# Second pass of a two-layer kernel: keys and values projected behind the unit's query, convolution taps dealt from one list of counts

## Chip, cores and metric

The kernel runs on one core of one Trainium2 chip, in float32. The time is device microseconds of one execution. Before the change three runs took 3788.51, 3795.89 and 3799.6 us, so the median is 3795.89 us.

## What is computed

Two layers follow each other on x of shape (8, 32, 32, 512).

```python
# layer 0: group norm, attention with 8 heads of 64 over 1024 tokens, output projection, residual
# layer 1, with B = 8 images of 1024 tokens and C = 512 channels:
q_img   = layernorm(x) @ wq + bq                        # as an image, channels first
o       = gelu(depthwise_conv7x7_stride2(q_img) + dw_b) # 16 x 16 points
points  = grid + tanh(conv1x1(o))                       # where to sample
smp     = bilinear_sample(x, points)                    # 256 samples of 512 channels
k = v   = smp @ wv + bv
kh, vh  = k @ mk_w + mk_b,  v @ mv_w + mv_b
qh      = q @ mq_w + mq_b
z       = softmax(qh kh^T) vh @ mo_w + mo_b + x         # 8 heads
out     = gelu(layernorm(z) @ mlp_w + mlp_b) + z
```

So in layer 1 an image's convolution must end before its samples can be gathered, and its samples before its keys and values are there. The chain of image b+1 runs while the attention of earlier images is computed.

## The kernel before, in words

**Two passes.** Layer 0 is the first pass; it ends some 2198 us into the profiled execution and is not touched. Layer 1 is the second pass (from line 776 on). There the projections of the reference are folded (`wvk`, `wvv`, `wqq`), and the work is cut into 64 **units**: image b has units 8b to 8b+7, for two halves of its tokens (`hi`) times four pairs of heads (`hp`).

**An order written out by hand.** Every step is put on a list with `at(place, step)` (line 347), where place is a unit's number and a fraction. `run_due` sorts by place and issues all steps in that order; `InOrder` keeps the program order on each engine. TensorE (PE), VectorE (DVE), ScalarE (ACT), GpSimd (POOL) and SyncE (SP, which issues DMAs) each run their own instructions in this order.

**A unit** n, in the order of its places:

- `scores` (n): 16 matmuls `sc<-keys,q`; DVE takes the negated maximum (`nmax<-sc`, two reductions), ACT the exponentials `e`. Then `product` of unit n-1 (`av<-et,vals`), `scale` (DVE, `attH`), and at n+0.17 `query_step` of the next unit (`mm<-hat_h,wqq`).
- From unit 4 on, the **tail of an earlier half**, one token tile t a unit (`back_steps`, line 1027): `joined` (`mm<-wo,attH`, then on DVE `z<-mm,xr`, `stats`, `mv`, with a power on POOL), `norm` (`zn`), `turned` (`mm<-ident,zn`), `mlp` (`mm<-wm,zT`), `biased` (DVE, `res<-mm,bm_row`), then for two tiles at a time Gelu on ACT and on POOL an addition and the store (`end`), followed by POOL's additions `xr<-xr,bo_row` (`add`) for the next two.
- `fill` (`mm<-wq_r,hat`): half a channel block of the query image; `fill_end` adds the bias into a padded image (`pad<-mm,bq_row`, on DVE). There are two padded images (`PADS`), used in turn by the four channel blocks of each image.
- `share` (DVE), the transposes `transposed` 0 and 1 (`mm<-ident,e`), `turn` (`mm<-ident,rep`).
- **Taps**: 49 multiply-adds a channel block, `o<-pad,dww,o`, all on DVE, 196 an image.

**PSUM.** All projections and transposes take their output from one ring of three tiles (`ps_mm`, line 268). The fourth allocation after a given one is issued only when the engine that empties the earlier tile has done so. Counted along a unit, the tile of `turned`, or of a key or value projection put ahead of it, is that of `fill`, which DVE empties with `pad<-mm,bq_row`.

**The steps that are moved.** `conv_steps` (line 1119) places fills and taps of image b over eight units, 8b-12 to 8b-5, in counts (23, 13, 29, 30, 28, 24, 25, 24); for b = 1 over units 0 to 3, 49 each. Then come Gelu, `offsets` (16 matmuls `mm<-pww,o`), `targets` (26 small DVE instructions), `gather` (four indirect DMAs from POOL, twice) and `sample` (four DVE instructions, twice). `key_step` (line 1007, `mm<-smp,wvk`, 8 matmuls) is placed four times at 8b-1.4, 8b-1.2, 8b+0.8 and 8b+2.2, `value_step` (line 1013, `mm<-wvv,smp`, 8 matmuls) twice at 8b-0.4 and 8b+0.6. In the order of PE these places lie between the transposes of e and `turned` (0.6), or between `mlp` and `turn` (0.8), except the one at 8b+2.2, which lies behind the query (n+0.17) and ahead of `joined` (n+0.46).

## Time and profile before

| | us |
|---|---|
| runs, median of three | 3795.89 |
| profiled execution, its own time | 3789.67 |
| its span in the trace | 3788.0 |
| TensorE busy over the span | 3578.3 |
| VectorE busy | 2789.1 |
| ScalarE busy | 1529.3 |
| GpSimd busy | 750.6 |
| units 0 to 3 (to the first matmul of unit 4) | 120.5 |
| units 4 to 13 | 246.8 |
| units 14 to 21 (and each eight after them, to unit 45) | 194.5 |
| units 46 to 51 | 150.7 |
| units 52 to 62 | 228.6 |
| unit 63 and the end | 64.5 |

A unit's length is the distance between the first `sc<-keys,q` matmuls of two units in the timeline of PE. Matmuls overlap, so work is best measured from start to start. A line of the timeline has the start, the length, the engine, the operation, what it writes and reads, the number of instructions in a run, and in brackets the idle time ahead of it with the instruction that ended it. In the view by stretches a row has the bounds, the length, then busy time and number of instructions for PE, PEld, DVE, ACT and POOL, the granted clock of TensorE, and the DMA share.

### The profile page before, as it was taken

The numbers are of one execution on the slowest core, as the hardware profiler recorded it, in microseconds if no ns is written. First come the engines' busy times: TensorE is split into PE (matmuls) and PEld (weight loads), VectorE is DVE, ScalarE is ACT, GpSimd is POOL, SyncE is SP. The second block draws the span as 40 slices with busy tenths as digits, with TensorE's granted clock in tenths as the row PEclk, the third lists the DMA queues.
The fourth block names the chain that finished last, engine by engine and source line by source line (L and its number), as shares of the span: only waits on it lengthen the run. The fifth ranks groups of instructions, "written<-read, shape, count | busy, mean of one in ns | idle before, by whom it ended". The sixth has DMA issues, their size and how long they took to land.

```text
span 3788.0 us, 46075 instructions
## 1 busy us (share of the span) xinstructions
PE 3578.3 (94%) x16152; PEld 1868.9 (49%) x16152; DVE 2789.1 (74%) x4264; ACT 1529.3 (40%) x3218; POOL 750.6 (20%) x838
## 2 busy tenths in 40 slices
PE   8999999999999999999998787999999999999997
PEld 4554554545545455455453434454545454544543
DVE  5678777776777777867766569898988888888333
ACT  3443443433434434344364123343434343444443
POOL 0003012020030120301346201121121212121212
PEclk9999999999999999999999898999999999999999
DMA  5667666665666666655755501021111111110100
GB/s 154 155 158 188 164 168 170 162 184 153 162 189 159 170 168 163 188 155 150 199 143 143 176 1 67 34 71 41 67 45 56 56 56 56 56 56 34 59 23 31
DMA packets 235350, 438.23 MB, mean 116 GB/s; under 512 B 49296, under 2 KB 53392, under 8 KB 232176
## 3 DMA queue, kind: packets, MB, share of 16 engines
q1 hardware_dynamic: 212528, 363.08, 35.4%
q0 software_dynamic: 21440, 70.11, 5.8%
q8 instruction: 129, 2.11, 0.2%
q10 hardware_dynamic: 1152, 2.10, 0.2%
q14 instruction: 101, 0.83, 0.1%
HBM read 115.84 MB, written 50.86 MB: 44 GB/s over the span
## 4 chain that ended last, share of the span: by engine, by line
PE 69%; DVE 20%; issue 6%; DMA 1%; ACT 1%; POOL 1%; SPq 0%; DVEq 0%; POOLq 0%; ACTq 0%
PE mm L53 42%; PE sc L53 15%; PE av L53 13%; DVE o L53 10%; DVE nmax L53 3%; DVE stats L53 1%; DVE sq L53 1%; DVE pad L53 1%; POOL mv L53 1%; ACT e L53 1%; DVE z L53 1%; DVE zn L53 1%; DVE attH L53 1%; DVE mv L53 1%; DMA row<-mid,ii 0%
## 5 line engine op out<-in xcount | busy, mean ns | idle before, releaser
L53 ACT ACTIVATE e<-sc,nmax 128x1024 f32<-128x1024 f32 (+1 forms) x1024 | 804.6, 799 | 901.8 <-DVE nmax L53 901.3
L53 DVE TENSOR_REDUCE nmax<-sc 128x1 f32<-128x1024 f32 (+1 forms) x640 | 753.2, 1219 | 481.5 <-PE sc L53 480.3
L53 DVE SCALAR_TENSOR_TENSOR o<-pad,dww,o 128x256 f32<-128x256 f32 x1344 | 721.3, 537 | 44.1
L53 DVE STREAM_TRANSPOSE sq<-e 128x1024 f32<-128x1024 f32 x512 | 608.1, 1226 | 50.8 <-ACT e L53 49.5
L53 PE MATMUL sc<-k,q 64*128 64x512 f32 x2048 | 527.3, 618 | 13.5 <-ACT q L53 6.2
L53 PE MATMUL av<-et,v 128*64 128x256 f32 x4096 | 504.2, 389 | 16.3 <-DMA et<-sq 9.4
L53 PE MATMUL mm<-xT,wqkv 128*128 128x512 f32 x1024 | 471.5, 604 | 2.6 <-issue 2.6
L53 PEld LDWEIGHTS av<-et,v 128*64 128x64 f32 x4096 | 276.0, 138 | 322.9 <-issue 177.2
L53 POOL TENSOR_TENSOR mv<-mv,minus_half 128x1 f32<-128x1 f32 x128 | 74.3, 581 | 1396.3 <-DVE mv L53 1334.1
L53 PEld LDWEIGHTS sc<-k,q 64*128 64x128 f32 x2048 | 181.6, 186 | 276.2 <-issue 229.8
L53 PEld LDWEIGHTS mm<-xT,wqkv 128*128 128x128 f32 x1024 | 185.9, 191 | 226.8 <-issue 219.7
L53 ACT COPY et<-mm 128x512 f32<-128x512 f32 x256 | 140.7, 593 | 317.6 <-PE mm L53 317.4
L53 PE MATMUL mm<-wqkv,xT 128*128 128x128 f32 x2048 | 244.5, 278 | 0.0
L53 PEld LDWEIGHTS mm<-wqkv,xT 128*128 128x128 f32 x2048 | 233.8, 192 | 19.9 <-issue 19.9
L53 PE MATMUL mm<-wm,zT 128*128 128x512 f32 x512 | 240.4, 613 | 2.9 <-ACT zT L53 2.9
L53 PE MATMUL mm<-hat_h,wqq 128*128 128x512 f32 x512 | 236.7, 605 | 0.0
L53 PE MATMUL mm<-wo,attH 128*128 128x512 f32 x512 | 231.4, 595 | 3.1 <-DVE attH L53 3.1
L53 PE MATMUL mm<-wout,attT 128*128 128x512 f32 x512 | 233.7, 601 | 0.0
L53 ACT ACTIVATION_READ_ACCUMULATOR e<-sc,nmax 128x1 f32 x1024 | 209.2, 204 | 0.0
L53 PE MATMUL mm<-wq_r,hat 128*128 128x512 f32 x448 | 203.8, 598 | 0.2 <-ACT et L53 0.2
L53 PE MATMUL mm<-ident,e 128*128 128x128 f32 x1024 | 152.6, 293 | 26.7 <-DVE z L53 11.4
L53 PEld LDWEIGHTS mm<-hat_h,wqq 128*128 128x128 f32 x512 | 92.1, 189 | 143.0 <-issue 131.6
(153 smaller groups left out, 3629.5 us busy)
## 6 DMA issues: line engine op xcount, KB each, us to landing
et<-sq SPq DMA_DIRECT2D x2048, 128.0 KB, 2.7
xr<-in_x_dram POOLq DMA_DIRECT2D x64, 256.0 KB, 3.7
hat_h<-hat_d SPq DMA_DIRECT2D x16, 1024.0 KB, 5.3
xr<-mid SPq DMA_DIRECT2D x64, 256.0 KB, 3.1
out_dram<-res POOLq DMA_DIRECT2D x64, 256.0 KB, 2.3
x<-in_x_dram POOLq DMA_DIRECT2D x60, 256.0 KB, 3.8
mid<-xr SPq DMA_DIRECT2D x56, 256.0 KB, 2.9
hat_d<-hat SPq DMA_DIRECT2D x56, 256.0 KB, 2.9
```

Of the source, the lines that this page charges most:

```text
L53: return self.tc.keep_in_program_order(op(*args, **kwargs))
```

## The change

The convolutions of all images get their places from one list of counts per unit: image 1 over five units (40, 40, 39, 39, 38), image 2 over seven (19, 26, 27, 27, 32, 32, 33), and images 3 to 7 over eight as before, in other counts. Fills take the last two free slots (n+0.49) ahead of a block's first tap. Where only one slot is free, both go into one unit, 0.26 apart. `point_steps` then places Gelu to sample by the unit in which the last tap stands (5 for image 1, 8b-4 for the others, as before). Keys go to 8b-1.82, 8b-1.81, 8b+1.18 and 8b+2.18, values to 8b-0.82 and 8b+0.18, that is right behind `query_step` in units 8b-2 (two keys), 8b-1 (value), 8b (value), 8b+1 (key), 8b+2 (key). For image 1 the first two keys come at 7.18. No instruction is added or removed.

```diff
-        def conv_steps(b):
-            last = 2 * NHP * b - NHP
-            each = 1 if b == 1 else 2
-            first = last - NC * each
...
-            for n, count in enumerate((49,) * NC if each == 1 else (23, 13, 29, 30, 28, 24, 25, 24)):
...
+        def conv_counts():
+            units = [40, 40, 39, 39, 38]
+            units += [19, 26, 27, 27, 32, 32, 33]
+            for _ in range(3, B):
+                units += [25, 13, 25, 31, 26, 28, 23, 25]
+            return units
...
+        def conv_steps():
+            chunks, filled = conv_places(), -2
+            for k, places in enumerate(chunks):
+                b, cb = 1 + k // NC, k % NC
+                if cb == 0 and b > 1:
+                    at(max(int(places[0]) - 2.45, filled + 0.02), lambda b=b: conv_fetch(b))
+                free = max(filled, chunks[k - PADS][-1] if k >= PADS else filled)
+                slots = [n + 0.49 for n in range(-1, 60) if free < n + 0.49 < places[0] - 0.05]
+                slots = slots[-2:] if len(slots) > 1 else [slots[0], slots[0] + 0.26]
+                filled = slots[1]
...
+                if cb == NC - 1:
+                    point_steps(b, int(places[-1]) + 1)
+
+        def point_steps(b, last):
             at(last - 0.035, lambda: conv_gelu(b))
...
-            for hp, place in enumerate((2.6, 2.8, 4.8, 6.2)):
-                at(last + place, lambda hp=hp: key_step(b, hp))
-            for t, place in enumerate((3.6, 4.6)):
-                at(last + place, lambda t=t: value_step(b, t))
+            first = 2 * NHP * b
+            for hp, place in enumerate((-1.82, -1.81, 1.18, 2.18)):
+                at(max(first + place, last + 2.18), lambda hp=hp: key_step(b, hp))
+            for t, place in enumerate((-0.82, 0.18)):
+                at(first + place, lambda t=t: value_step(b, t))
...
-        for b in range(1, B):
-            conv_steps(b)
+        conv_steps()
```

Within a unit the taps keep their fractions: 45% of a unit's count between 0.26 and 0.46, which is ahead of `joined` on DVE, the rest behind `share`.

More of the change, by code (lines that the diff above doesn't have):

```diff
@@ L1117, in unit_steps, with conv_places @@
                 at(n + 0.17, lambda: query_step(*divmod(n + 1, NHP)))
-        def conv_steps(b):
-            last = 2 * NHP * b - NHP
-            each = 1 if b == 1 else 2
-            first = last - NC * each
-            if b > 1:
-                at(first - 2.45, lambda: conv_fetch(b))
-            for cb in range(NC):
-                for par in range(2):
-                    n, frac = divmod(par * each, 2)
-                    n = first + cb * each - each + (par if each == 2 else 0)
-                    frac = 0.49 if each == 2 or par == 0 else 0.75
-                    if (b, cb) == (2, 0):
-                        n, frac = first - 1, 0.49 + 0.3 * par
-                    at(n + frac, lambda cb=cb, par=par: fill(b, cb, par))
-                    at(n + frac + 0.04, lambda cb=cb, par=par: fill_end(cb, par))
-            i = 0
-            for n, count in enumerate((49,) * NC if each == 1 else (23, 13, 29, 30, 28, 24, 25, 24)):
+        def conv_counts():
[4 more added lines that the diff above has]
+            return units
+        def conv_places():
+            places = []
+            for n, count in enumerate(conv_counts()):
                 for j in range(count):
@@ L1141, in conv_steps @@
                     x = 0.26 + 0.2 * x / 0.45 if x < 0.45 else 0.57 + 0.36 * (x - 0.45) / 0.55
-                    at(first + n + x, lambda i=i: tap(b, *divmod(i, KS * KS)))
-                    i += 1
+                    places.append(n + x)
+            taps = KS * KS
+            return [places[i : i + taps] for i in range(0, len(places), taps)]
+        def conv_steps():
[8 more added lines that the diff above has]
+                filled = slots[1]
+                for par, place in enumerate(slots):
+                    at(place, lambda b=b, cb=cb, par=par: fill(b, cb, par))
+                    at(place + 0.04, lambda cb=cb, par=par: fill_end(cb, par))
+                for i, place in enumerate(places):
+                    at(place, lambda b=b, cb=cb, i=i: tap(b, cb, i))
+                if cb == NC - 1:
+                    point_steps(b, int(places[-1]) + 1)
+        def point_steps(b, last):
             at(last - 0.035, lambda: conv_gelu(b))
```

## Prediction

> **What bounds the kernel now.** First the page: which engine is full, and where.

> ```profile
> PE 3578.3 (94%) x16152; PEld 1868.9 (49%) x16152; DVE 2789.1 (74%) x4264; ACT 1529.3 (40%) x3218; POOL 750.6 (20%) x838
> ...
> DVE  5678777776777777867766569898988888888333
> ...
> PEclk9999999999999999999999898999999999999999
> ```

> The second pass is the last 17 slices. VectorE is at 8 to 9 tenths there and drops to 3 when the convolutions are done; TensorE stays near 9. Two engines are close to full, so the question is how they wait for each other. Next the stretches (units 0 to 3, 14 to 21, 53 to 62):

> ```profile
> 2198.50:2319.00 120.50, 88.10 (x281) 44.06 (x280) 105.00 (x208) 27.96 (x87) 2.88 (x2) 0.85 0.09 35
> ...
> 2565.90:2760.40 194.50, 184.06 (x707) 97.64 (x706) 169.36 (x323) 80.35 (x211) 38.13 (x40) 0.98 0.16 55
> ...
> 3515.80:3723.40 207.60, 191.20 (x769) 103.32 (x768) 69.73 (x119) 98.11 (x256) 42.67 (x46) 0.98 0.12 41
> ```

> Units 0 to 3 are VectorE's, the last ones TensorE's, and in the eight units that repeat both are nearly full, TensorE with 10.4 us idle. Then PE's timeline of unit 14, the longest of the eight (30.6 us), and DVE's beside it:

> ```profile
> 2576.64 3.60 PE L53 MATMUL mm<-wq_r,hat 128*128 128x512 f32 x8
> 2580.07 0.60 PE L53 MATMUL mm<-ident,e 128*128 128x128 f32 x4
> 2581.93 0.66 PE L53 MATMUL mm<-ident,e 128*128 128x128 f32 x4 [1.26 <-DVE z L53]
> 2584.88 3.78 PE L53 MATMUL mm<-smp,wvk 128*128 128x256 f32 x8 [2.29 <-DVE pad L53]
> 2588.46 1.05 PE L53 MATMUL mm<-ident,zn 128*128 128x128 f32 x4
> ```

> ```profile
> 2570.77 10.24 DVE L53 SCALAR_TENSOR_TENSOR o<-pad,dww,o 128x256 f32<-128x256 f32 x13
> ...
> 2581.19 0.68 DVE L53 TENSOR_TENSOR z<-mm,xr 128x512 f32<-128x512 f32 x1
> ...
> 2584.14 0.68 DVE L53 TENSOR_TENSOR pad<-mm,bq_row 128x512 f32<-128x512 f32 x1
> ```

> The key projection stands where its PSUM tile is the fill's, and waits until DVE, behind 14 taps, has emptied it. Without the key, `turned` would wait for the same `pad`. So the key is work that TensorE has in hand and does after the wait instead of before it. The view of waits puts 49.1 us in 34 places on `pad` from unit 4 on.

> **Durations, from start to start.** All from PE's and DVE's timelines of units 12 to 20. A tap costs 0.513 (16 in 8.2), but even units lose 3.2 more: from 2570.77 to `z` at 2581.19 14 taps took 10.42 where 7.2 are due, because POOL's second store addition and its two `add`s (2.7 to 9.6 us into the unit) each hold a tap up; if taps start after 6.2, only the `add`s remain, 2.4. Key 1.82, value 3.54, `offsets` 1.70, targets 3.1, one `sample` 2.76. PE reaches `joined` at 7.33, `fill` ends at 14.36, `turned` would start at 15.15, and from `turned` to the unit's end 5.40 pass. On DVE, nmax starts at 2.03 or when the unit before is finished (its lag d); taps start 2.87 later; `z` to the start of `pad` 2.95; `turned` follows `pad` by 0.74; the second part of the taps by 1.17, and `res` ends DVE's unit after 0.60 more.

> With these few terms I walk along both queues unit by unit: `z` = nmax + 2.87 + taps (or `joined`, if later), `pad` = z + 2.95 (or the fill, if later), `turned` = the later of TensorE's own place and pad + 0.74. For units 12 to 19 before the change the walk gives 192.1; measured 194.5. The rest is the halved clock in unit 14, where a key took 3.58 instead of 1.82 and the unit 2.6 more than walked. So the walk holds to 1 us in eight units.

> **1. Keys and values behind the query, units 14 to 45.** Each puts `joined`, `fill` and `turned` back by its own length and gives DVE that time. The walk for the new counts:

> - unit 12 (25 taps, offsets): lag 2.3, `pad` 17.5, `turned` 18.2 for a place of 16.85; length 23.6, lag after it 5.4
> - 13 (13 taps, two samples): `pad` 17.1, `turned` 17.8 for 15.15; 23.2
> - 14 (two keys): `turned` at its own place 18.79, no wait; 24.2 (was 30.6)
> - 15 (value): 18.69, no wait; 24.1 (24.7), lag 4.3 from 31 taps
> - 16 (value, 12 + 14 taps): z = 4.3 + 2.87 + 12 x 0.513 + 2.4 = 15.8, `pad` 18.7, `turned` 19.5 for 15.15 + 3.54 = 18.69; length 19.5 + 5.4 = 24.9 (29.1); lag 18.7 + 1.17 + 14 x 0.513 + 0.6 - 24.9 = 2.8
> - 17 (key): 16.97, no wait; 22.4 (20.6)
> - 18 (key): 17.9 for 16.97; 23.3 (23.6)
> - 19: no wait; 20.55 (20.57)

> The sum is 186.2. The wait in unit 13, 2.65, is put at half clock for one window, 1.7: 187.9 for 194.5, so 6.6 less, four times: **-26.4**. The instructions moved are 48 matmuls and six evacuations on ACT per image; they queue behind the query's evacuation, done 5.7 us after nmax starts, when ACT is idle for 4 us. A key behind the query (7.33) takes the tile of `res` of the unit before, so it would wait for DVE beyond a lag of 7.3; the walk's largest is 5.4. DMAs of these steps: none.

> [...]

> ```profile
> 2580.20:2583.60 3.40, 1.13 (x9) 0.65 (x7) 2.67 (x7) 1.17 (x2) 0.51 (x1) 1.00 0.17 62
> 2634.80:2638.20 3.40, 1.85 (x10) 0.92 (x8) 2.74 (x7) 1.17 (x2) 0.40 (x1) 1.00 0.00 0
> 3611.00:3614.40 3.40, 1.15 (x11) 0.91 (x10) 2.60 (x7) 1.07 (x2) 0.55 (x1) 1.00 0.24 77
> ```

> After the first and third, a third busy, the clock is 0.5; after the second, 54% busy, it stays; no single gap is over 2.3. So I count about 2.05 us idle within one 3.4 us window as the limit, and unit 13 falls under it. [...]

> **2. Units 46 to 51.** The same up to 49 (24.2, 24.1, 24.9, 22.4); 50 and 51, without fills, stay at 24.4 and 20.3: 140.3 for 150.7, **-10.4**.

> **3. Units 52 to 62, a loss.** There are no fills and taps, and `turned` waits for `zn`, which follows `joined` at a fixed distance. A key or value between the two covers that wait:

> ```profile
> 3589.09 3.71 PE L53 MATMUL mm<-wvv,smp 128*128 128x512 f32 x8
> ...
> 3613.89 0.66 PE L53 MATMUL mm<-ident,zn 128*128 128x128 f32 x4 [2.25 <-DVE zn L53]
> ```

> Moved ahead of `joined`, it no longer does: units 54, 55 and 56 get the wait of 2.3. A unit is then 19.42, ten of them 194.2, four keys and two values 14.4, halved clock in four or five (3 of 7 such units before) 7.2: 215.8 for 207.6, **+8.2**. [...]

> **4. Units 0 to 13.** DVE sets the pace at first: nine taps fewer a unit (4.65) and a `pad` (0.6) fewer in two units bring unit 4's nmax from 2331.7 to 2311.9. But 38 taps of image 1 are left, with two fills in that unit: the second comes behind `mlp`, and its `pad` makes DVE wait about 4.3, and the next query 1.2 for the tile of `res`. From there the walk gives 23.5, 28.7, 27.7, 24.7, 22.5, 28.5, 25.3, 25.0, 24.9 for units 5 to 13: 6 (z = 2.1 + 2.87 + 12 x 0.513 + 2.76 + 3.2 = 17.1, `turned` 20.8 for 15.15) and 10 stand 5.7 and 4.0 us on DVE and get the halved clock (2 to 2.5 each, as unit 4), 7 is PE's (two keys and a value), 11 has two fills again. Unit 4 ends at 2339.2, so unit 14 starts at 2570.0 for 2565.9: **+4.1**. Nothing near shows such units, so from both sides: without halved clocks -5, with two windows each +11. I take +4.1, since unit 14's row, with 3.55 idle, did halve. The image's fetch (8 us to land) now waits in SP's queue for unit 3's second fill, 2299, and lands at 2307, ahead of its fill at 2316; behind it in that queue are only row fetches for unit 5. Unit 5's gathers stand ahead of POOL's additions, which end at 11.5 of unit 6; `z` comes at 17.

> **Sum.** -26.4 - 10.4 + 8.2 + 4.1 = -24.5. Span 3788.0 gives 3763.5, the profiled execution 3789.67 gives 3765.2, and the median of the runs 3795.89, 6 above it, gives 3771.4; I say 3771.

> **Rivals.** (a) *VectorE stays behind* (chance 0.15): the lag isn't worked off, because POOL holds up 3.2 in every even unit. Then units 16 and 18 get 0.8 each, lag into 13 makes 0.5, and the clock halves for two windows: 191.5 per eight, -12.0; 46 to 51 -7; tail and beginning +12 and +11: +4, 3800. For it: DVE's 169.4 busy plus some 13 of small gaps and POOL waits is 183 of 186. Against: the same walk meets before. (b) *Slower by the clock* (0.07): from 2.05 us idle in one window on, half clock; if units 12, 13 and 18 all pass it, with two windows (3.3) each, each eight lose 9.9 instead of 1.7: 5 x 8.2 = +41, and if all ten tail units halve, +9.5. That is +26, 3822. For it: unit 12 has offsets and 1.4 us idle close together. Against: unit 18 waits 0.9 only. (c) *More* (0.13): the beginning gives -5, the tail halves nowhere (+1), and 13 doesn't either: -26.4 - 6.8 - 10.4 + 1 - 5 = -48, 3748. That the new counts gain nothing of themselves is no rival: it is step 4 of the forecast, which has 0.65.

> **Numbers.** The forecast's own range is 3757 to 3784, from the beginning's ends (-9, +7) and 1 us for each eight. With most of (a) and (c): 3750 to 3790. No change means within 0.3%, 11.4 us, about what a measurement here can tell. Faster by more: (c), and 0.64 of the forecast's 0.65: 0.77. Within: the 0.01 left and 0.14 of (a): 0.15. Slower: (b) and the rest of (a): 0.08.

> **What would show it.** Units 14 and 16 near 24 to 25, without `DVE pad` ahead of `mm<-smp,wvk`; units 17 longer by 1.8; unit 13 with the longest wait of the eight; units 54 to 56 with `DVE zn` 2.3; nmax of unit 4 near 2312 and unit 14's start near 2570. Wrong if waits on `res` stand ahead of keys, or if unit 14 still shows 0.5 clock.

## Result and the profile after

| | before | after |
|---|---|---|
| median of the runs, us | 3793.72 (six, 3781.4 to 3799.6) | 3751.95 (six, 3743.9 to 3755.47) |
| profiled execution, its own time | 3789.67 | 3752.78 |
| its span | 3788.0 | 3751.1 |

The ratio is 0.9894, with a 95% interval of 0.9879 to 0.991: faster by 1.1%. By the medians that is 41.8 us, by the spans 36.9 us; the difference is that the profiled execution of before lay 4.1 below the median of its six runs, and that of after 0.8 above its own. The forecast was 3771 (24.5 less), with a range of 3750 to 3790. The direction held, and the median lies 2 us inside the short end of the range: the gain is 1.7 times the one forecast.

The first lines of the page of after:

```profile
PE 3561.1 (95%) x16152; PEld 1862.0 (50%) x16152; DVE 2784.0 (74%) x4264; ACT 1528.0 (41%) x3218; POOL 748.9 (20%) x838
...
DVE  5678677776787777767866749898989899998333
...
PEclk9999999999999999999999988999999999999999
```

The number of instructions is the same on every engine. TensorE's busy time is 17 less although it does the same work: the records of the granted clock have half clock for 187.2 us of the span before and 154.1 after, and a matmul at half clock counts as longer busy (the first key of unit 14 took 3.58 before, from start to start, and takes 1.81 now). So the page alone tells little; the stretches tell more (units 0 to 3, 14 to 21, 53 to 62; the last column is what the DMAs moved, in GB/s):

```profile
2197.90:2300.40 102.50, 77.20 (x267) 39.55 (x266) 88.14 (x172) 27.82 (x87) 2.83 (x2) 0.88 0.05 17
2565.50:2751.60 186.10, 182.11 (x705) 96.93 (x704) 168.24 (x323) 80.15 (x211) 38.07 (x40) 0.99 0.16 57
3470.70:3689.40 218.70, 195.77 (x771) 107.06 (x770) 69.86 (x119) 98.86 (x256) 42.55 (x46) 0.95 0.11 39
```

Units 0 to 3 are 18.0 shorter, units 14 to 21 are 8.4 shorter, and 53 to 62 are 11.1 longer at a lower clock. In the eight that repeat, TensorE's idle time went from 10.4 to 4.0 and its busy time from 184.06 to 182.11. Unit 14 on PE shows how:

```profile
2569.28 3.70 PE L53 MATMUL mm<-hat_h,wqq 128*128 128x512 f32 x8
2572.82 3.79 PE L53 MATMUL mm<-smp,wvk 128*128 128x256 f32 x16
2576.44 3.59 PE L53 MATMUL mm<-wo,attH 128*128 128x512 f32 x8
2579.87 3.60 PE L53 MATMUL mm<-wq_r,hat 128*128 128x512 f32 x8
2583.31 1.04 PE L53 MATMUL mm<-ident,e 128*128 128x128 f32 x8
2584.25 0.66 PE L53 MATMUL mm<-ident,zn 128*128 128x128 f32 x4
```

The two keys are one run of 16 behind the query, with no bracket anywhere: nothing in this unit waits. Before, the first key stood behind the transposes with 2.29 of idle time ahead of it, and its eight matmuls took 3.58 for 1.81. The unit is now 24.20, from 30.64. The view of waits of PE from unit 4 on (total, times, longest), where `pad` had 49.1 in 34 places:

```profile
PE mm L53 <- DVE zn L53: 39.3, 17, 4.4
PE mm L53 <- DVE pad L53: 24.7, 19, 2.3
PE mm L53 <- DVE z L53: 8.2, 3, 4.4
```

Half of the waits on `pad` are gone. Those on `zn` rose from 26.0 to 39.3: that is the price, and it falls in the head and in the tail.

### The profile page after: what moved, and what is told of

It reads as the page before. It is cut to its first block, busy times and chain, and to the rows that moved or that the text cites. A ratio compares the mean times of both kernels' runs of the same rounds, so it can differ in the third digit from the quotient of the medians.

```text
span 3751.1 us, 46076 instructions
## 1 busy us (share of the span) xinstructions
PE 3561.1 (95%) x16152; PEld 1862.0 (50%) x16152; DVE 2784.0 (74%) x4264; ACT 1528.0 (41%) x3218; POOL 748.9 (20%) x838
## 4 chain that ended last, share of the span: by engine, by line
PE 73%; DVE 17%; issue 6%; POOL 1%; ACT 1%; DMA 1%; SPq 0%; DVEq 0%; POOLq 0%; ACTq 0%
PE mm L53 45%; PE sc L53 14%; PE av L53 13%; DVE o L53 8%; DVE nmax L53 2%; DVE stats L53 1%; DVE sq L53 1%; ACT e L53 1%; DVE pad L53 1%; POOL mv L53 1%; DVE z L53 1%; DVE smp L53 0%; DMA row<-mid,ii 0%; DVE zn L53 0%; DVE mv L53 0%
## 5 line engine op out<-in xcount | busy, mean ns | idle before, releaser
L53 ACT ACTIVATE e<-sc,nmax 128x1024 f32<-128x1024 f32 (+1 forms) x1024 | 803.6, 798 | 902.7 <-DVE nmax L53 898.8
L53 DVE TENSOR_REDUCE nmax<-sc 128x1 f32<-128x1024 f32 (+1 forms) x640 | 752.8, 1218 | 426.1 <-PE sc L53 425.0
L53 DVE SCALAR_TENSOR_TENSOR o<-pad,dww,o 128x256 f32<-128x256 f32 x1344 | 718.6, 535 | 43.9
L53 DVE STREAM_TRANSPOSE sq<-e 128x1024 f32<-128x1024 f32 x512 | 608.2, 1226 | 50.5 <-ACT e L53 49.3
L53 PE MATMUL sc<-k,q 64*128 64x512 f32 x2048 | 527.3, 618 | 13.5 <-ACT q L53 6.2
L53 PE MATMUL av<-et,v 128*64 128x256 f32 x4096 | 502.8, 388 | 15.9 <-DMA et<-sq 9.0
L53 PE MATMUL mm<-xT,wqkv 128*128 128x512 f32 x1024 | 471.5, 604 | 2.6 <-issue 2.6
L53 PEld LDWEIGHTS av<-et,v 128*64 128x64 f32 x4096 | 275.3, 137 | 321.7 <-issue 177.0
L53 POOL TENSOR_TENSOR mv<-mv,minus_half 128x1 f32<-128x1 f32 x128 | 74.0, 578 | 1409.8 <-DVE mv L53 1341.2
L53 PEld LDWEIGHTS sc<-k,q 64*128 64x128 f32 x2048 | 181.6, 186 | 276.2 <-issue 230.6
L53 PEld LDWEIGHTS mm<-xT,wqkv 128*128 128x128 f32 x1024 | 185.9, 191 | 226.7 <-issue 219.7
L53 ACT COPY et<-mm 128x512 f32<-128x512 f32 x256 | 140.4, 594 | 320.1 <-PE mm L53 319.8
L53 PE MATMUL mm<-wm,zT 128*128 128x512 f32 x512 | 243.4, 619 | 2.9 <-ACT zT L53 2.9
L53 PE MATMUL mm<-wqkv,xT 128*128 128x128 f32 x2048 | 244.5, 278 | 0.0
L53 PEld LDWEIGHTS mm<-wqkv,xT 128*128 128x128 f32 x2048 | 233.8, 192 | 19.9 <-issue 19.9
L53 PE MATMUL mm<-hat_h,wqq 128*128 128x512 f32 x512 | 236.7, 605 | 0.0
L53 PE MATMUL mm<-wo,attH 128*128 128x512 f32 x512 | 231.4, 594 | 3.5 <-DVE attH L53 3.5
L53 PE MATMUL mm<-wout,attT 128*128 128x512 f32 x512 | 233.7, 601 | 0.0
L53 ACT ACTIVATION_READ_ACCUMULATOR e<-sc,nmax 128x1 f32 x1024 | 209.2, 204 | 0.0
L53 PE MATMUL mm<-wq_r,hat 128*128 128x512 f32 x448 | 203.1, 596 | 0.2 <-ACT et L53 0.2
L53 ACT COPY inv<-mm 128x512 f32<-128x512 f32 x128 | 74.3, 580 | 254.1 <-PE mm L53 250.6
L53 PE MATMUL mm<-ident,e 128*128 128x128 f32 x1024 | 149.7, 293 | 16.6 <-DVE z L53 8.2
```

The costliest lines, as they stand in the source:

```text
L53: return self.tc.keep_in_program_order(op(*args, **kwargs))
```

## Where each stretch went

| stretch | before | forecast | after | change forecast | change measured |
|---|---|---|---|---|---|
| units 0 to 13 (step 4) | 367.4 | 371.5 | 367.5 | +4.1 | +0.1 |
| units 14 to 45 (step 1) | 778.2 | 751.8 | 744.6 | -26.4 | -33.6 |
| units 46 to 51 (step 2) | 150.7 | 140.3 | 139.5 | -10.4 | -11.2 |
| units 52 to 62 (step 3) | 228.7 | 236.9 | 239.8 | +8.2 | +11.1 |
| unit 63 and the end | 64.5 | 64.5 | 61.7 | 0 | -2.8 |

The sum is -36.4, and the second pass starts 0.6 earlier, which makes the 36.9 of the spans.

## Experiments

**Theory.** The whole gain comes from the places of keys and values; the new counts add nothing in the eights that repeat, cost some in units 4 to 13, and the same places lose in the tail. **Rival:** the counts bring the gain, as they work DVE's lag off, and the places only move a wait.

All medians are set against runs of the kernel before on the same chip (its medians lie between 3790.05 and 3790.85 in the experiments' groups, at 3793.72 in that of after). Stretches are those of the profiled execution, with the sum of the second pass last:

| kernel | median | ratio (95%) | 0-13 | 14-45 | 46-51 | 52-62 | 63 | sum |
|---|---|---|---|---|---|---|---|---|
| before | | | 367.4 | 778.2 | 150.7 | 228.7 | 64.5 | 1589.5 |
| after | 3751.95 | 0.9894 (0.9879-0.991) | 367.5 | 744.6 | 139.5 | 239.8 | 61.7 | 1553.1 |
| e1 places only | 3742.97 | 0.9879 (0.986-0.9898) | 358.8 | 743.6 | 142.8 | 238.0 | 63.2 | 1546.4 |
| e2 counts only | 3783.71 | 0.9983 (0.9976-0.9989) | 376.1 | 768.4 | 150.4 | 232.0 | 64.4 | 1591.3 |
| e3 last image back | 3742.43 | 0.9884 (0.986-0.9908) | 366.8 | 744.6 | 139.5 | 228.8 | 64.6 | 1544.3 |
| e4 old counts, images 1, 2 | 3746.68 | 0.9889 (0.9868-0.9909) | 360.1 | 744.7 | 139.6 | 239.6 | 61.8 | 1545.8 |
| e5 = e3 and e4 | 3740.05 | 0.9859 (0.9843-0.9875) | 361.6 | 750.9 | 142.6 | 228.8 | 64.6 | 1548.5 |
| e6 behind the fill | 3730.54 | 0.9839 (0.9823-0.9856) | 360.6 | 744.3 | 138.1 | 222.7 | 61.8 | 1527.5 |
| e7 no addition on POOL | 3720.24 | 0.9816 (0.9799-0.9832) | 357.6 | 726.1 | 135.4 | 239.4 | 62.2 | 1520.7 |
| e8 old counts, behind the fill | 3732.55 | 0.9847 (0.983-0.9863) | 359.4 | 744.3 | 142.9 | 222.6 | 61.8 | 1531.0 |
| e9 fewer taps in 12 and 13 | 3751.19 | 0.9886 (0.9864-0.9907) | 359.3 | 764.8 | 144.1 | 224.5 | 63.1 | 1555.8 |
| e10 counts, fills unmoved | 3717.25 | 0.9803 (0.9786-0.982) | 357.9 | 732.8 | 138.7 | 222.8 | 61.8 | 1514.0 |
| e11 after, once more | 3756.84 | 0.9911 (0.9894-0.9928) | 367.5 | 744.7 | 139.5 | 239.8 | 61.7 | 1553.2 |

The first pass, which no kernel touches, differs between profiled executions by up to 7 us (it ends at 2192.8 in e3, at 2199.9 in e6), so stretches are the finer measure. e11 repeats every stretch of after to 0.1 us, and its median to 0.13%. Not every stretch is held so well by one trace: e4 and e5 issue the same instructions in the same order up to unit 53, and their units 14 to 45 took 744.7 and 750.9. A difference of 6 us there can be the clock's alone; e5 below shows how.

**e1, places only.** The old counts, and the new places on top of them:

```diff
-            for hp, place in enumerate((2.6, 2.8, 4.8, 6.2)):
+            for hp, place in enumerate((2.18, 2.19, 5.18, 6.18)):
...
-            for t, place in enumerate((3.6, 4.6)):
+            for t, place in enumerate((3.18, 4.18)):
```

> The kernel before with only the new places of keys and values; counts of taps and places of fills stay as they were. Theory (the gain is that keys and values stand ahead of the wait for the fill's tile; the new counts give little): units 14 to 21 at 185 to 186 us, as in the changed kernel, unit 54 to 58 lengthened by 10 in all, and units 6 to 13 some 8 shorter, so 40 to 44 us less than before, about 3751, the changed kernel's time. Rival (the counts carry the gain): within 10 us of before, units 14 to 21 above 190.

Measured 3742.97. Six numbers carry the whole gain, and the trace says no less: units 14 to 45 are 743.6 against 744.6 in the changed kernel, units 0 to 13 are 358.8 for 367.5, for the old counts repeat the pattern of units 14 to 17 in units 6 to 9, and the places shorten those too.

**e2, counts only.** The changed kernel with the old places:

```diff
-            for hp, place in enumerate((-1.82, -1.81, 1.18, 2.18)):
+            for hp, place in enumerate((-1.4, -1.2, 0.8, 2.2)):
...
-            for t, place in enumerate((-0.82, 0.18)):
+            for t, place in enumerate((-0.4, 0.6)):
```

> The changed kernel with keys and values at their old places (those of image 1 not ahead of its samples); counts and fills are the new ones. Theory: the wait for the fill's tile is back ahead of the key in units 14 and 16, units 14 to 21 at 191.5 to 194 us, the time within 8 us of before, 3786 to 3796. Rival (counts carry the gain): 30 us or more of the 42 stay, 3765 or less.

Measured 3783.71, 6.3 less than before (the profiled execution was the longest of its 20 runs, so its sum is no measure of the gain). In unit 14 the wait is back ahead of the key, and the key takes 3.40 from start to start, where the second one of that unit takes 1.82:

```profile
2588.84 0.66 PE L53 MATMUL mm<-ident,e 128*128 128x128 f32 x4 [0.20 <-DVE z L53]
2591.78 3.56 PE L53 MATMUL mm<-smp,wvk 128*128 128x256 f32 x8 [2.29 <-DVE pad L53]
```

Of the two idle times that unit 14 had before, the counts shorten only the one on `z` (1.26 to 0.20). The effects do not add: in these traces counts alone take 9.8 from units 14 to 45 (the four eights of e2 are 194.1, 192.5, 190.9 and 190.9), places alone 34.6, both 33.6. What the counts save is a part of the wait that the places remove. The rival falls.

**e3, the last image back.** The changed kernel, but image 7's keys and values at the old places:

```diff
-            for hp, place in enumerate((-1.82, -1.81, 1.18, 2.18)):
+            for hp, place in enumerate((-1.82, -1.81, 1.18, 2.18) if b < B - 1 else (-1.4, -1.2, 0.8, 2.2)):
...
-            for t, place in enumerate((-0.82, 0.18)):
+            for t, place in enumerate((-0.82, 0.18) if b < B - 1 else (-0.4, 0.6)):
```

> The changed kernel with the last image's keys and values alone at their old places, where no fills are left. Theory (there they covered the wait for zn): units 54 to 58 lose the wait of 2.3 three times and some halved clock, 9 to 12 us less than the changed kernel, 3740 to 3743; units 12 to 51 to the tenth as in it, but for 54 on. Rival (the loss in units 52 to 62 is the clock's phase alone): within 4 us of the changed kernel.

Units 52 to 62 are 228.8, as before the change: 11.0 taken back in the trace, 9.5 by the medians. So the loss in this stretch is these six steps and nothing else. The last stretch goes the other way, though: unit 63 and the end are 64.6 with the steps back and 61.7 with them moved, so the tail's net loss is 8.1. In the changed kernel unit 55 shows it, with the value `wvv,smp` ahead of `joined` and nothing between the transposes and `turned`:

```profile
3522.31 3.60 PE L53 MATMUL mm<-wvv,smp 128*128 128x512 f32 x8
3525.74 3.60 PE L53 MATMUL mm<-wo,attH 128*128 128x512 f32 x8
3529.18 1.04 PE L53 MATMUL mm<-ident,e 128*128 128x128 f32 x8
3532.47 0.66 PE L53 MATMUL mm<-ident,zn 128*128 128x128 f32 x4 [2.25 <-DVE zn L53]
```

**e4, old counts for images 1 and 2.**

```diff
-            units = [40, 40, 39, 39, 38]
-            units += [19, 26, 27, 27, 32, 32, 33]
+            units = [49, 49, 49, 49]
+            units += [23, 13, 29, 30, 28, 24, 25, 24]
```

> The changed kernel with the old counts for images 1 and 2 (49 each over four units, eight units for image 2); new places and the other counts stay. Theory (dealing image 1 over five units and image 2 over seven costs as much as it gives, by two fills in one unit twice and half clock in units 4, 6, 10, 12): unit 14 starts some 7 us earlier than in the changed kernel, at 2557 to 2560 of its own trace, the time 3743 to 3747. Rival (the dealing of images 1 and 2 is part of the gain): 5 us or more above the changed kernel.

Units 0 to 13 are 360.1 for 367.5, the rest is unchanged. By the medians the 5.3 lie inside the intervals; the traces have them: units 0 to 13 are 366.8 to 367.5 in after, e3 and e11, and 360.1 and 361.6 in e4 and e5, which have the old counts for images 1 and 2. So the five and seven units of the first two images, which make units 0 to 3 18.0 shorter, give back more than that: they cost 7.4 to unit 13. Two views of unit 4 of the changed kernel show where, first PE, then DVE:

```profile
2326.24 1.08 PE L53 MATMUL mm<-ident,zn 128*128 128x128 f32 x4 [4.41 <-DVE zn L53]
...
2333.17 3.60 PE L53 MATMUL mm<-wq_r,hat 128*128 128x512 f32 x8
```

```profile
2327.18 6.21 DVE L53 SCALAR_TENSOR_TENSOR o<-pad,dww,o 128x256 f32<-128x256 f32 x12
2336.81 0.69 DVE L53 TENSOR_TENSOR pad<-mm,bq_row 128x512 f32<-128x512 f32 x1 [3.42 <-PE mm L53]
```

TensorE waits 4.41 for `zn`, which stands on DVE behind 18 taps of image 1 (9.3 us); then DVE waits 3.42 for the second fill of the same unit, which stands behind `mlp` on TensorE. Each waits for the other once, and the unit takes 36.76.

**e5, e3 and e4 together.**

> The changed kernel with both parts that lost taken back: old counts for images 1 and 2, and the last image's keys and values at their old places. Theory (the parts add up): 7 us less in units 0 to 13 and 11 less in units 52 to 62 than the changed kernel, 3732 to 3738 where the changed kernel has 3752. Rival (what is gained in one part is given back by the clock or the queues in the next): 3742 or more.

Measured 3740.05, between theory (up to 3738) and rival (from 3742), with two runs on either side: 3734.03 and 3736.02, 3744.08 and 3746.34. By the medians it is 11.9 below the changed kernel, where e3 gave 9.5 and e4 5.3; the 2.9 that are missing lie inside the intervals. The trace, of the longest of the four runs, misses more: 1548.5, where the gains of e3 and e4 would make 1537.0. Units 13, 21 and so on show where: the same wait of 2.2 as in the changed kernel, at another price. Unit 21 of e5, by PE's timeline and by two windows of 3.4 us:

```profile
2735.10 1.04 PE L53 MATMUL mm<-ident,e 128*128 128x128 f32 x8
2738.37 1.11 PE L53 MATMUL mm<-ident,zn 128*128 128x128 f32 x4 [2.24 <-DVE pad L53]
```

```profile
2734.90:2738.30 3.40, 1.23 (x9) 0.80 (x7) 2.61 (x7) 1.07 (x2) 1.65 (x3) 1.00 0.63 199
2738.30:2741.70 3.40, 3.33 (x13) 2.96 (x14) 3.22 (x9) 1.64 (x3) 0.00 (x0) 0.51 0.00 1
```

And unit 29 of the changed kernel:

```profile
2928.00:2931.40 3.40, 2.20 (x12) 1.20 (x10) 2.58 (x7) 1.07 (x2) 2.60 (x3) 1.00 0.60 176
2931.40:2934.80 3.40, 2.38 (x15) 1.86 (x16) 3.26 (x8) 1.57 (x3) 0.00 (x0) 1.00 0.20 64
```

In e5 the wait falls into one window (PE 1.23 of 3.40 busy), and the next one has a clock of 0.51; in after it is split over two (2.20 and 2.38), and the clock stays at 1.00. The unit is 24.44 there and 22.86 here. So the same wait cost 1.6 in one trace and nothing in the other, and what differs is its phase, that is, where in the windows it falls. The edit did not set that phase, for e4, with the same instructions up to unit 53, has eights of 186.2 where e5 has 187.7. The records of the granted clock in the traces of before and after (58 each) start whole multiples of 3.413 us apart: that is the window meant here. In after the two records of half clock in units 14 to 45 (units 20 and 36) stand 372.05 apart, 109 windows for two eights, so an eight is 54.5 of them and the eights meet them in two ways by turns. The 187.7 of e5 is 55.0, so by the author's estimate every eight of e5 meets them in the same way. One trace would then hold the sum of units 14 to 45 only to some 6 us (four eights of 1.6), again an estimate. Whether the two shorter runs of e5 had the better phase is not shown.

**e6, behind the fill.** Keys and values not behind the query but one place later, between `fill` and the transposes (counts of e4):

```diff
-            for hp, place in enumerate((-1.82, -1.81, 1.18, 2.18)):
+            for hp, place in enumerate((-1.5, -1.499, 1.5, 2.5)):
...
-            for t, place in enumerate((-0.82, 0.18)):
+            for t, place in enumerate((-0.5, 0.5)):
```

> Old counts for images 1 and 2, the changed kernel's other counts, and every key and value placed directly behind the fill (n+0.5) and ahead of the transposes of e, instead of behind the query. Theory (what counts is only that TensorE has this work in hand before it needs the tile that DVE empties, and a key behind the query holds up the fill and with it pad): unit 16 loses its wait of 1.5, units 14 to 21 at 185 to 186 us, and since the place is also between joined and the transposed zn, units 54 to 58 keep their cover; 3728 to 3736. Rival (the place behind the query matters, since it gives DVE time before joined): the wait for pad returns in units 14 and 16, units 14 to 21 at 189 us or more, 3745 or more.

Measured 3730.54, 16.1 less than e4, from which it differs by these six places alone. What a value behind the query costs is seen on DVE in unit 15 of the changed kernel, with the maximum of unit 16 below it, and then on PE in unit 16:

```profile
2604.08 0.69 DVE L53 TENSOR_TENSOR z<-mm,xr 128x512 f32<-128x512 f32 x1 [2.03 <-PE mm L53]
...
2618.99 2.35 DVE L53 TENSOR_REDUCE nmax<-sc 128x4 f32<-128x1024 f32 x2
```

```profile
2633.88 0.66 PE L53 MATMUL mm<-ident,zn 128*128 128x128 f32 x4 [1.52 <-DVE pad L53]
```

The same in e6:

```profile
2596.93 0.69 DVE L53 TENSOR_TENSOR z<-mm,xr 128x512 f32<-128x512 f32 x1
...
2610.91 2.36 DVE L53 TENSOR_REDUCE nmax<-sc 128x4 f32<-128x1024 f32 x2 [0.45 <-PE sc L53]
```

```profile
2619.65 3.60 PE L53 MATMUL mm<-wq_r,hat 128*128 128x512 f32 x8
2623.08 3.60 PE L53 MATMUL mm<-wvv,smp 128*128 128x512 f32 x8
2626.51 1.04 PE L53 MATMUL mm<-ident,e 128*128 128x128 f32 x8
2627.39 0.63 PE L53 MATMUL mm<-ident,zn 128*128 128x128 f32 x4
```

Behind the query, the value puts `joined` back by its own 3.5, and DVE, done with its taps, stands 2.03 for it: `z` comes 14.4 into unit 15. That time is missing later: DVE takes unit 16's maximum 5.3 into the unit, its `pad` is late, and `turned` waits 1.52. Behind the fill, `joined` and the fill stay early, `z` comes at 12.0 without a wait, the maximum of unit 16 at 2.0, and the value runs while DVE makes `zn` and `pad`. Unit 16 is 24.01 for 25.59. In the tail the cover is kept: units 54 to 58 are 20.77, 20.58, 20.57, 19.52 and 19.60, and the stretch is 222.7, less than before the change. By the traces 16.9 of the 18.3 that e6 has over e4 lie there. The sum of the eights hardly moves (744.3 for 744.7): what unit 16 gains goes again, 0.2 in unit 14, 0.5 in unit 18, and in the first and third eight in their last unit (unit 21 is 24.49, near the 24.44 of e5's halved one; the eights are 186.9, 185.2, 186.9, 185.4).

**e7, no addition on POOL.** The changed kernel without `xr += bo_row` in `add`: the output bias is left out of z.

```diff
             def add(t):
-                nc.gpsimd.tensor_tensor(xr[t], xr[t], bo_row, ALU.add)
+                pass
```

> The changed kernel without POOL's addition of the output bias to the residual tile (xr), so the bias is left out of the result. Theory (these two additions in each even unit each hold a tap up, 2.4 us of DVE together, and DVE is what the waits left in units 12, 16 and 18 stand on): the taps ahead of z in even units lose 2 to 2.4 us, the waits in units 16 and 18 are gone, that in 12 nearly, units 14 to 21 at 182 to 183 us, the time 3724 to 3732. Rival (the waits left come from the counts and the chain z to pad, POOL's additions run beside the taps): units 14 to 21 stay at 186, 3748 to 3755.

Measured 3720.24, 31.7 less than the changed kernel by the medians, a bit more than expected; units 14 to 21 are 181.5. The four taps ahead of `z` in unit 16 on DVE, in after and in e7, and between them POOL in after at that time:

```profile
2621.85 4.51 DVE L53 SCALAR_TENSOR_TENSOR o<-pad,dww,o 128x256 f32<-128x256 f32 x4
```

```profile
2622.01 2.50 POOL L53 TENSOR_TENSOR xr<-xr,bo_row 128x512 f32<-128x512 f32 x2
```

```profile
2609.62 2.04 DVE L53 SCALAR_TENSOR_TENSOR o<-pad,dww,o 128x256 f32<-128x256 f32 x4
```

The first of the four taps lasts 2.95 in after, until both additions are done, where a tap takes 0.485. By the profile it starts 0.16 ahead of the first addition and ends 0.29 after the second. Of the 1372 taps of after, the 1316 beside which no 512-wide addition runs on POOL take at most 0.50, and the 56 others take up to 2.97. In the walk this is the term of 2.4 in z. Without it the waits of units 16 and 18 are gone (24.01 and 22.39 for 25.59 and 23.02).

**e8, all old counts, behind the fill.** e6 with 23, 13, 29, 30, 28, 24, 25, 24 for images 3 to 7 too.

> All counts as before the change, and every key and value directly behind the fill (n+0.5). Theory (the counts hardly matter once the keys stand ahead of the wait): units 14 to 21 at 185 to 187 us, the time within 4 us of the run with the new counts and the same places, 3729 to 3738. Rival (with 29 and 28 taps in units 14 and 16 DVE is late again, and the new counts are needed): 8 us or more above that run.

3732.55 against 3730.54: between these two lists of counts there is no difference at these places. Units 14 to 21 are 186.1.

**e9, fewer taps in units 12 and 13.** e6 with other counts for images 3 to 7, to take the waits of 12 and 13 away:

```diff
-                units += [25, 13, 25, 31, 26, 28, 23, 25]
+                units += [22, 11, 26, 32, 27, 29, 23, 26]
```

> Keys and values behind the fill, old counts for images 1 and 2, and for images 3 to 7 the counts (22, 11, 26, 32, 27, 29, 23, 26) instead of (25, 13, 25, 31, 26, 28, 23, 25): fewer taps in the two units that also hold targets and samples, where the waits are left (1.2 and 2.2, and half clock in 13). Theory (DVE's lag out of unit 12, not its sum, makes these waits): unit 12 without a wait, unit 13 with 1.0 to 1.3 and full clock, the taps taken up in 14 to 19 for at most 0.8 more wait in unit 18: units 14 to 21 at 183 to 185 us for 186.9, the time 3716 to 3726. Rival (DVE is full over the eight units, so a wait only moves): units 14 to 21 at 186 or more, 3727 to 3734.

Measured 3751.19, units 14 to 21 191.3: theory and rival both missed. PE's timeline of units 15 and 16 shows what I had overlooked:

```profile
2588.62 3.60 PE L53 MATMUL mm<-wq_r,hat 128*128 128x512 f32 x8
...
2601.33 3.60 PE L53 MATMUL mm<-wq_r,hat 128*128 128x512 f32 x8
...
2622.93 0.60 PE L53 MATMUL mm<-ident,e 128*128 128x128 f32 x4
2625.49 0.79 PE L53 MATMUL mm<-ident,e 128*128 128x128 f32 x4 [1.96 <-DVE pad L53]
```

The counts also set where blocks begin and end, and so in which units the fills fall. Here two fills fall into unit 15 (27.44 for 24.01) and none into unit 12. A list of counts is a schedule of matmuls as well.

**e10, counts that leave the fills where they are.** e6 with a list that leaves each fill in its unit:

```diff
-                units += [25, 13, 25, 31, 26, 28, 23, 25]
+                units += [17, 19, 29, 33, 24, 31, 20, 23]
```

> As the run with fewer taps in units 12 and 13, but with counts that leave every fill alone in the unit where it stood: (17, 19, 29, 33, 24, 31, 20, 23) for images 3 to 7; keys and values behind the fill, old counts for images 1 and 2. Theory (that run lost by two fills in unit 15 and none in unit 12, and what is left in the eight units is DVE's lag out of unit 12): unit 12 without a wait, 13 and 14 with about 1.2 to 1.4, no halved clock in the eight; units 14 to 21 at 183 to 184.5 us, the time 3716 to 3724. Rival (fewer taps in unit 12 lose whatever the fills do, DVE is full): units 14 to 21 at 187 or more, 3731 or more.

Measured 3717.25, ratio 0.9803 (0.9786 to 0.982): faster than both kernels, and 39.6 less than the changed one on the same chip (e11, 3756.84). Units 14 to 21:

```profile
2555.00:2738.20 183.20, 181.06 (x705) 95.36 (x704) 167.01 (x323) 80.17 (x211) 38.09 (x40) 1.00 0.17 58
```

The expectation was 183 to 184.5. By PE's timeline unit 14 waits 0.41 and 0.87 and unit 21 0.86, the rest not at all; the clock is 1.00 throughout, and TensorE is busy for all but 2.1. So counts do matter at these places: e6, e9 and e10 differ in nothing but the list (in e9 with the fills that it moves) and lie between 3717 and 3751.

**e11, the changed kernel once more**, on the chip of e10.

> The changed kernel itself, beside the run with the re-dealt counts on the same chip, to compare the two: 3748 to 3756 by every theory, units 14 to 21 at 186.2.

Its median, 3756.84, is just above what was expected; all its stretches are those of the first profile.

## Why the prediction was right in kind and short in size

**The mechanism held.** The key was work that TensorE had in hand and did after the wait; put ahead of it, the wait went. The signs are there: units 14 and 16 are 24.20 and 25.59 (24.2 and 24.9 forecast) with no wait ahead of a key, units 54 to 56 have the wait of 2.3 on `zn`. Unit 17 is 22.39 (22.4), 15 is 24.01 (24.1), 18 is 23.02 (23.3), 19 is 20.57 (20.55). No wait on `res` stands ahead of a key. That the eight came out to a tenth is in part luck: unit 16 took 0.7 more than walked, the other seven together 0.8 less.

**Step 1, -26.4, measured -33.6.** The term that was mis-sized is the half clock of unit 13, put at 1.7 an eight, 6.8 in four. The walk without it said 186.2; each eight measured 186.1 or 186.2. The wait itself is there (2.2 for 2.65), but it was priced by its length alone, and in these traces its cost went by its phase. In two eights it fell across two windows (2.20 and 2.38 of 3.40 busy in unit 29) and cost nothing; in the other two the clock halved one unit earlier, in 20 and 36, where unit 20 took 25.00 for 23.5. That gave VectorE time, so unit 21's wait shrank to 0.7 and its length to 21.37: 46.4 for both, as in units 28 and 29. So a half clock just ahead of a wait on another engine cost nothing here, since the wait took it up. In e5's trace, with the same steps in these units, the four eights took 750.9, as if each had paid 1.6: -27.3, where -26.4 was forecast. Of the 7.2 by which the forecast missed, then, nearly all is the luck of the phase, as far as these two traces tell. The kernel before may hold as much: its records of half clock stand 194.56 apart from unit 14 to unit 46, 57.0 windows, so each of its eights met the windows alike, and no run tells what another phase would have made of them.

**Step 4, +4.1, measured +0.1.** The way of the loss was as told (unit 4 with two fills, DVE waiting 3.42 for the second; units 6 to 11 within 0.6 of the forecast: 29.01, 27.63, 24.12, 22.39, 28.82, 25.26). Unit 4's nmax came at 2310.9 (2311.9), unit 5 began at 2337.1 (2339.2) and took 22.31 (23.5). Units 12 and 13 were forecast at 49.9 and took 48.8, 28.23 with half clock and 20.57 after it, again a half clock that the next unit took up. And the two parts that this stretch sums are larger than the sum suggests: places -8.6 (e1), counts +8.7 (e2). That the counts lose so much in the beginning by themselves was not seen. So the small sum is two larger parts that cancel.

**Step 3, +8.2, measured +11.1.** The waits are where they were put. Six of the ten units at the end (54, 56, 58, 59, 61 and 62) had the half clock, where four or five were taken: 1.6 or so each (unit 61 took 21.07, unit 60 without it 19.53).

**Step 2, -10.4, measured -11.2**, within 1. Units 50 and 51 were said to stay at 24.4 and 20.3; before the change they were 24.58 and 21.06, and they came out at 23.80 and 19.50.

**Unit 63, 0, measured -2.8:** its clock is 0.94 for 0.90. The table ties this to image 7's steps: the stretch is 64.4 to 64.6 in the four kernels that have them at the old places (before, e2, e3, e5), and 61.7 to 63.2 in all others. The prediction has nothing on this stretch; how these steps reach unit 63's clock is not shown. With it the tail is 8.3 longer, by chance near the +8.2 of step 3 alone.

**The rivals.** VectorE staying behind (3800) did not come: the lag was worked off as the walk said. Slower by the clock (3822) did not come: no eight has more than one half clock (two records of it in units 14 to 45). "More" (3748) was nearest in time, yet only its part on unit 13 was true: the tail did halve, and the beginning did not gain 5. What the prediction did not ask is whether the edit's two halves were both needed. They were not: by e1 the places alone give as much.

**What stays open.** Why the clock halved after the windows with `offsets` in units 12, 20, 36 and 52 is answered below only by comparing windows; no run here measures these matmuls by themselves. What sets the phase in which an execution meets the windows was not found.

## What to carry to other kernels

Where two nearly full engines hand tiles to each other in order, look for work that an engine has in hand and does after a wait, and put it between request and answer: behind the last step that the other engine waits for (here `fill`), not ahead of the first, where it delays the request itself. Unit 16 shows the delay, though most of what e6 gained came from the cover in the tail. A step moved to where it covers a wait in one stage can uncover one in another, so price the stage without the feature (the tail) by itself. When counts or places are computed from one list, see what else that list moves before changing a number in it.

## What was not expected of the hardware

```profile
2719.80:2723.20 3.40, 2.44 (x22) 2.20 (x21) 2.63 (x6) 1.25 (x3) 0.55 (x1) 1.00 0.01 2
2723.20:2726.60 3.40, 3.21 (x13) 2.96 (x14) 3.19 (x9) 1.52 (x3) 0.00 (x0) 0.50 0.00 0
```

  Fourteen of the sixteen lie in this window and take 1.51 us; the other matmuls alone fill 1.07 of it, 0.31. In the two traces 25 windows at full clock hold such matmuls. Without them, the five that were followed by half clock are busy for 0.31 to 0.46 of the time and the other 20 for 0.48 or more; with them, the five have 0.52 to 0.91. From these figures the author's estimate is that such narrow matmuls counted for little or nothing here. It was not measured alone.
- Of the 56 taps of after that overlap a 512-wide addition on POOL, 47 end only 0.16 to 0.29 after it, or after the second of two: one in unit 16 lasts 2.95, where 0.485 is usual. The 64 additions of this kind, 81 us of POOL's busy time, cost 31.7 us (e7).
